# A four-layer gated attention and expert kernel: stacked masks in layer 0, half of the softmax sums in pairs on GpSimd, and a new planned order

## The chip, the cores and the metric

The kernel runs on one core of one Trainium2 chip. The core has five engines that run at the same time, each in the order of its own queue: TensorE (PE in the profile; its weight loads are the row PEld), VectorE (DVE), ScalarE (ACT), GpSimd (POOL) and SyncE (SP), which issues most of the transfers. The metric is the device time of one execution in microseconds (us), the median of several runs.

## The reference

There are 16 sequences of 128 tokens of width 128, and a context of 77 rows for each. Four layers follow each other, each an attention to the context and a feed-forward part, both gated into the token:

```
x = x + tanh(g_xattn[0]) * L0_xattn(layernorm(x), ctx, fside, mask)   # 16 heads of 8
x = x + tanh(g_ffn[0])   * L0_ffn(layernorm(x))                       # 8 experts, threshold router with capacity
x = x + tanh(g_xattn[1]) * L1_xattn(layernorm(x), ctx, key_mask)      # 16 heads of 8
x = x + tanh(g_ffn[1])   * L1_ffn(layernorm(x))                       # expert 0, layer norm
x = x + tanh(g_xattn[2]) * L2_xattn(layernorm(x), ctx)                # 16 heads of 64
x = x + tanh(g_ffn[2])   * L2_ffn(layernorm(x))                       # quantized
x = x + tanh(g_xattn[3]) * L3_xattn(layernorm(x), ctx, key_mask)      # 8 heads of 64
x = x + tanh(g_ffn[3])   * L3_ffn(layernorm(x))                       # 8 experts, best one for each token
```

Layer 0's attention, in short: the scores of a query with the 77 keys of its sequence get -1e9 where the mask (one value for each query and key) is 0. Their softmax is multiplied with `fside`, a weight for each query and key, and then with the values. The softmax divides by the sum of the exponents before that weighting. Layer 1's attention is alike, with a mask by keys and without the weighting.

Layer 0's router: a token's experts are ranked by their probability, those up to a mass of 0.9 are chosen, and each expert keeps the 256 tokens with the best value of probability less rank.

## The kernel before

The 16 sequences ("batches" here) are worked on in four groups of four. In `small_group` (layers 0 and 1) a group goes through a layer norm, a transposition, a product for its queries and one for its keys. Then, for each batch, `scores` (L820, L824) fills four strips of 128 queries x 308 (four heads of 77 keys) in PSUM. Each strip takes the mask terms first and then the product of queries and keys. Layer 0 has two mask terms for each strip: a 128x128 diagonal of 30512 and one of 5.578125, both half precision, times `pen0`, which is 0 or -32768 (L1190 makes it of the loaded mask). So a batch has eight mask products and four products of queries and keys, of two instructions each (L824).

The two halves of a batch's 16 heads then go each through: the maximum over the keys (L632), the difference (L634), the exponent (L839, ScalarE), in layer 0 the weighting with `fside` (L856, GpSimd or VectorE), and the sum over the keys (L844, VectorE, 8 heads x 77 keys). The sums of both halves together are inverted (L847), spread (L867), turned (L871) and copied (L875). The exponents, weighted in layer 0, are turned by TensorE in blocks of 128 (L650), copied back, and multiplied with the values (L885). That product is scaled with the inverted sums (L890), projected (L894) and added to the token (L693). The values pass through memory on their way (L793 stores, L797 loads), on SP's queue.

`norm` is the layer norm that all layers use: statistics on VectorE (L491), a few small instructions on GpSimd (`moments`, L498 to L503), two on ScalarE (L508, L510), again a few on GpSimd (`newton`, L514 to L520), and the scaling of the group's four batches on ScalarE (L526) or VectorE (L528).

`route_part` computes layer 0's routing of a group on VectorE: ranks (L1562 to L1571), the value that decides (L1572 to L1577), and its spreading over 16 columns (L1582) ahead of a transposition.

Other work fills the gaps of layer 0: the products of value and output weights with the context (L1486), which layers 2 and 3 need, and the keys of these layers (L1649).

All of this is written as pieces of work with a due time, an engine (or two to choose from, with a cost for each) and what each reads and writes. `Work.layout` plays the pieces through with these costs and writes them out in the order in which they would start. The order of every engine's queue, and the choice of engine, follows from that. `NUDGES` is a list of (first piece, number of pieces, hundredths) that moves due times, and `SLACK` makes VectorE look dearer by 0.5 in a choice. At run time an engine that reaches an instruction whose inputs aren't ready waits there.

Of the kernel before, what the change touches and what calls it, by code (L numbers as in the profile page):

```python
# [11 lines left out]
F32 = mybir.dt.float32  # L12
F16 = mybir.dt.float16
# [9 lines left out]
P = 128  # L23
B = 16
D = 128
# [34 lines left out]
WEIGH, WEIGH_COST = ("POOL", "DVE"), (1.3, 0.85)  # L60
SIDE, SIDE_COST = ("POOL", "DVE"), (1.3, 0.75)
# [12 lines left out]

NUDGES = (
    (206, 1, 230), (1755, 1, 143), (2153, 1, -200), (2640, 4, 268), (963, 1, -150), (960, 4, -257), (1701, 1, 117), (1797, 3,
    -30), (989, 1, -212), (1726, 8, -153), (2228, 4, 172), (2164, 2, -283), (1712, 1, -267), (1001, 1, -283), (1670, 6,
    -289), (1652, 1, -189), (813, 1, -237), (164, 8, -58), (162, 2, -260), (879, 6, 267), (1136, 1, -206), (141, 4, -145),
    (130, 1, 220), (738, 6, -165), (2242, 4, -104), (961, 1, -103), (2244, 8, -295), (1770, 2, 104), (488, 8, 333), (1339, 1,
    65), (466, 8, 69), (611, 4, 133), (1771, 1, -214), (65, 1, -226), (137, 4, -273), (2126, 1, -231), (567, 1, -156), (991,  # L80
    1, -231), (2046, 4, 47), (1919, 6, -283), (2452, 4, 299), (2195, 1, 100), (689, 1, -177), (1805, 2, 116), (332, 8, -352),
    (337, 8, -46), (956, 3, -22), (749, 8, -114), (2053, 8, 58), (2559, 1, -190), (501, 8, 217), (2655, 8, -72), (1935, 1,
    -263), (1015, 1, -100), (2403, 1, -88), (2766, 8, 120), (18, 8, 217), (399, 1, -14), (1548, 4, -46), (1542, 6, -252),
    (2445, 4, -44), (397, 8, 38), (849, 8, -70), (961, 1, -99), (1914, 2, -52), (1530, 4, -250), (869, 4, 264), (392, 1,
    156), (2068, 6, -52), (852, 4, 92), (1693, 2, -62), (991, 3, -232), (611, 8, 89), (869, 1, -276), (801, 1, 281), (2196,
    8, -30), (2416, 6, -273), (2216, 1, -248), (867, 5, -264), (2514, 5, -30), (798, 1, -157), (2351, 2, -317), (2685, 8,
    -69), (1474, 1, -91), (2385, 1, 256), (1690, 1, -24), (2175, 1, 121), (2054, 4, -47), (2514, 4, 127), (1485, 8, 274),
    (392, 2, 72), (2542, 6, -186), (1806, 8, 89), (987, 5, -196), (2633, 3, -250), (492, 8, -236), (406, 1, -183), (1838, 4,
    -210), (2352, 1, 274), (2199, 1, -277), (1610, 6, -212), (2547, 1, 242), (1723, 4, 60), (1676, 1, 271), (2059, 8, -270),
    (268, 8, -210), (1753, 8, 42), (2631, 2, -107), (1547, 1, -182), (1579, 4, 19), (377, 1, -73), (2080, 1, -38), (465, 1,  # L90
    -122), (2636, 3, 278), (995, 3, -161), (1571, 8, -123), (751, 1, -281), (249, 4, -311), (2634, 8, -121), (854, 6, 175),
    (798, 1, 75), (2614, 8, -397), (2289, 1, -240), (1009, 1, -99), (2536, 4, -99), (1299, 1, -270), (1024, 4, -270), (741,
    1, -114), (2480, 1, -296), (2417, 2, -257), (761, 1, -284), (2254, 2, -218), (971, 2, -251), (1011, 4, -314), (2837, 8,
    252), (1936, 4, 186), (2111, 8, -333), (1853, 1, 135), (600, 8, -33), (1839, 1, -241), (1855, 5, -100), (940, 1, -191),
    (769, 5, -205), (2002, 8, -31), (781, 4, -32), (756, 1, 62), (1072, 8, 12), (755, 2, -156), (2636, 2, 106), (1983, 8,
    -341), (1339, 1, -80), (1386, 1, -266), (859, 1, -136), (1416, 8, 137), (46, 4, 380), (756, 1, 143), (758, 1, -131),
    (1391, 2, 150), (2561, 1, -293), (940, 1, -187), (1841, 4, -270), (1507, 1, 86), (1946, 8, 10), (981, 1, -279), (446, 6,
    -301), (2680, 1, -210), (1864, 1, 190), (737, 2, -81), (1015, 1, 241), (1552, 3, 189), (2717, 4, -126), (18, 5, -237),
    (1001, 2, 288), (1022, 1, 163), (2195, 1, -59), (2536, 5, 258), (2458, 4, -80), (2490, 1, -296), (2494, 6, -198), (1560,
    4, -287), (1911, 5, -16), (864, 1, -297), (149, 3, 221), (1876, 4, 273), (1434, 4, -304), (2206, 3, -140), (41, 8, 260),  # L100
    (1443, 8, -98), (2206, 8, 75), (2039, 5, -256), (2046, 1, -229), (922, 1, -228), (985, 1, -170), (2074, 1, -269), (1418,
    4, -275), (2793, 5, -298), (2718, 4, -126), (1507, 1, -302), (869, 6, 233), (2206, 1, -48), (2034, 1, -65), (2068, 1,
    -220), (1851, 1, -301), (748, 4, 118), (1397, 8, 143), (1507, 1, 286), (1514, 1, -260), (375, 1, -253), (985, 1, -152),
    (2206, 1, -42), (2252, 1, -231), (1746, 8, 119), (2306, 1, 78), (1467, 6, -111), (1633, 1, 72), (1952, 1, -186), (981, 1,
    172), (411, 2, -92), (559, 8, 123), (397, 4, -18), (1219, 1, -151), (2480, 2, 127), (852, 1, -203), (1613, 2, 294),
    (2670, 8, -326), (2256, 1, -242), (953, 1, -194), (1058, 8, 100), (1952, 1, -49), (532, 1, -164), (1048, 4, -80), (1054,
    8, -91), (741, 1, -138), (2249, 8, 400), (987, 6, -205), (367, 6, -265), (803, 8, 294), (1414, 2, -267), (2897, 8, -243),
    (2492, 3, -282), (963, 1, 115), (1633, 1, -57), (1509, 1, -97), (1041, 2, 306), (806, 1, -238), (2008, 1, -88), (975, 1,
    -260), (920, 8, -208), (258, 8, -230), (491, 8, -48), (874, 1, -300), (607, 2, -81), (945, 1, -271), (789, 3, -171),
    (460, 1, 24), (791, 4, 298), (258, 2, 336), (741, 1, -71), (689, 1, -288), (2897, 4, 388), (1005, 1, -266), (959, 1,  # L110
    -21), (857, 1, 92), (431, 3, -191), (934, 1, -104), (801, 1, 296), (851, 4, -164), (854, 4, -222), (1851, 1, -94), (993,
    5, -152), (2101, 1, -233), (971, 1, 279), (972, 2, -204), (254, 1, -202), (1940, 8, -90), (869, 1, 75), (973, 1, -112),
    (1794, 3, -141), (2592, 4, -114), (973, 4, -248), (859, 6, -286), (2470, 1, -271), (1570, 2, -115), (533, 4, 282), (961,
    1, -279), (46, 8, -174), (969, 1, -122), (1612, 3, -61), (971, 2, -134), (2242, 5, 240), (2114, 8, -331), (1575, 4,
    -325), (2897, 4, -181), (2095, 4, -171), (276, 1, 275), (969, 1, -211), (1042, 1, -131), (1896, 4, 108), (969, 8, -121),
    (763, 1, -263), (2099, 3, -38), (2206, 4, -65), (1000, 4, -204), (2357, 4, 299), (579, 4, -325), (662, 3, -236), (2856,
    8, -367), (484, 8, 218), (2161, 1, -159), (223, 2, -98), (1570, 1, -262), (244, 8, -158), (222, 8, 52), (2175, 4, 50),
    (1503, 4, -114), (2473, 8, 89), (1843, 8, 137), (2215, 6, -274), (139, 1, 191), (1004, 6, -159), (748, 1, -271), (1838,
    4, -140), (2849, 1, 134), (999, 1, -226), (985, 4, -245), (2798, 5, -220), (922, 4, -286), (1052, 2, 119), (928, 5,
    -300), (981, 1, -222), (740, 8, -110), (1612, 4, -84), (1015, 2, -88), (996, 8, -105), (44, 8, -95), (2461, 5, 205),  # L120
    (1502, 4, -117), (2221, 4, -226), (485, 4, -357), (297, 4, -110), (1050, 4, -134), (2813, 1, -122), (1709, 1, -130),
    (1613, 8, 134), (2448, 8, 230), (969, 1, -243), (1004, 4, -257), (763, 1, -222), (2778, 4, 99), (2470, 8, 194), (689, 1,
    -221), (852, 4, -204), (741, 1, -194), (981, 1, -125), (1202, 6, -239), (894, 1, -144), (2159, 1, -243), (1609, 8, -138),
    (1466, 4, -384), (961, 1, -177), (991, 3, -168), (2474, 1, -277), (1057, 3, -180), (502, 1, -127), (2777, 5, 273), (1895,
    4, -78), (965, 5, -74), (995, 1, -230), (854, 4, -281), (154, 2, 382), (2206, 2, 85), (753, 2, -288), (2215, 6, -253),
    (969, 8, -361), (745, 4, 83), (974, 5, -239), (923, 6, -261), (983, 1, -186), (879, 1, 71), (625, 1, -169), (981, 1,
    -132), (140, 5, -185), (1802, 4, 47), (481, 8, 253), (2304, 2, -132), (1801, 5, -82), (2388, 6, 296), (743, 4, -136),
    (983, 6, 97), (872, 6, 146), (949, 5, -17), (865, 5, 90), (925, 5, -181), (136, 5, -180), (778, 1, -78), (803, 1, -263),
    (368, 1, 208), (2837, 8, 354), (1228, 1, 115), (2206, 1, -65), (1058, 1, -151), (793, 1, -302), (643, 1, 276), (2205, 3,
# [27 lines left out]
class Work:  # L157
# [50 lines left out]
    def nudged(self):  # L208

        due = [n["at"] for n in self.nodes]  # L210
        for first, count, hundredths in NUDGES:
            for i in range(first, min(len(due), first + count)):
                due[i] += hundredths / 100.0
# [1865 lines left out]
```

## Time and profile before

| | |
|---|---|
| median of 3 runs | 663.42 us (663.17 to 665.4) |
| the profiled execution | 666.49 us, span 664.8 us |
| mean granted TensorE clock | 0.976 |
| transfers | 117.47 MB, 177 GB/s over the span |

The span runs from the first instruction to the last; the execution's own time has 1.7 us more around it. A row of a group of instructions gives line, engine, operation, output and input with their shapes and the number of instructions, then the busy time and the mean duration of one in ns, then the idle time of the engine just before them and what ended it. Of the rows that the change touches, the difference (L634) and the maximum (L632) are the largest of VectorE: 112 instructions of 799 ns and of 780 ns.

### The profile page before, as it was taken

How to read it: one execution, taken by the hardware profiler on the slowest of the kernel's cores; microseconds unless marked ns; L12 is line 12 of the kernel's file. 1: busy time of each engine (PE TensorE's matmuls, PEld its weight loads, DVE VectorE, ACT ScalarE, POOL GpSimd, SP SyncE). 2: the span in 40 equal slices, each digit the busy share in tenths (PEclk: the TensorE clock that was granted, in tenths of full speed). 3: DMA queues.
4: the chain of work that ended last, by engine and by line, in shares of the span. 5: the costliest groups of instructions: out<-in, count | busy, mean ns of one | idle time of the engine just before them, and what ended most of it. 6: DMA issues, size and time to landing. Idle time of an engine off the chain costs nothing.

```text
span 664.8 us, 16370 instructions
## 1 busy us (share of the span) xinstructions
PE 604.2 (91%) x5795; PEld 435.4 (65%) x5795; DVE 524.9 (79%) x1224; ACT 427.2 (64%) x1131; POOL 305.8 (46%) x750
## 2 busy tenths in 40 slices
PE   3988998899999999988989999999999998799795
PEld 2555565565546778655646776687767776689795
DVE  3699999884675347999998998979999999878342
ACT  3545758577766656686687867647686758356463
POOL 8659445351000027624362735445445347645554
PEclk9888999999999999998999999999999999799898
DMA  8972473557445565489592757569964432666473
GB/s 228 272 233 68 150 183 110 150 165 207 144 131 159 160 187 144 140 239 296 160 269 88 217 169 227 188 175 315 292 178 130 122 98 83 198 180 181 125 225 84
DMA packets 169178, 117.47 MB, mean 177 GB/s; under 512 B 12649, under 2 KB 159984, under 8 KB 169098
## 3 DMA queue, kind: packets, MB, share of 16 engines
q1 hardware_dynamic: 166650, 112.55, 59.6%
q0 software_dynamic: 1728, 3.17, 1.3%
q8 instruction: 46, 0.75, 0.5%
q10 hardware_dynamic: 720, 0.71, 0.4%
q14 instruction: 34, 0.28, 0.1%
HBM read 61.43 MB, written 55.89 MB: 176 GB/s over the span
## 4 chain that ended last, share of the span: by engine, by line
PE 29%; DVE 13%; ACT 7%; POOL 7%; issue 2%; DMA 1%; another core or an unknown queue 1%; DVEq 0%; ACTq 0%; POOLq 0%
PE T L650 4%; PE h_ps L1927 4%; PE y L1001 4%; PE y L1942 3%; DVE pr L634 3%; PE q_ps L931 3%; DVE mx L632 2%; PE y L1062 2%; POOL pw L995 2%; PE h_ps L1041 2%; PE S L975 1%; DVE sb L988 1%; ACT xn L526 1%; PE O L885 1%; DVE ln_st L491 1%
## 5 line engine op out<-in xcount | busy, mean ns | idle before, releaser
L634 DVE TENSOR_TENSOR pr<-S,mx 128x616 f32<-128x616 f32 x112 | 89.5, 799 | 6.7
L632 DVE TENSOR_REDUCE mx<-S 128x8 f32<-128x616 f32 x112 | 87.4, 780 | 4.8 <-PE S L824 4.0
L650 PE MATMUL T<-ident,pw 128*128 128x128 f32 (+1 forms) x400 | 63.0, 284 | 6.5 <-POOL pw L995 4.3
L463 ACT COPY pT<-T 128x384 f32<-128x384 f32 x107 | 50.5, 479 | 26.6 <-PE T L650 26.0
L995 POOL TENSOR_TENSOR pw<-pr,rinv 128x616 f32<-128x616 f32 x34 | 41.2, 1216 | 53.5 <-DVE rinv L990 10.4
L650 PEld LDWEIGHTS T<-ident,pw 128*128 128x128 f32 (+1 forms) x400 | 45.9, 142 | 29.1 <-issue 12.0
L1001 PEld LDWEIGHTS y<-v,pT 128*128 128x128 f32 (+1 forms) x480 | 57.8, 191 | 9.6 <-issue 4.0
L1001 PE MATMUL y<-v,pT 128*128 128x128 f32 (+1 forms) x480 | 62.1, 278 | 1.5 <-ACT pT L463 1.1
L839 ACT ACTIVATE pr<-pr 128x616 f32<-128x616 f32 x64 | 45.9, 720 | 20.3 <-DVE pr L634 20.1
L856 POOL TENSOR_TENSOR pw<-pr,gp 128x616 f32<-128x616 f32 x26 | 36.0, 1387 | 37.2 <-ACT pr L839 23.9
L1811 DVE SCALAR_TENSOR_TENSOR token<-y,sc,token 128x128 f32<-128x128 f32 x96 | 32.9, 349 | 24.2 <-PE y L1806 21.7
L844 DVE TENSOR_REDUCE ss<-pr 128x8 f32<-128x616 f32 x64 | 49.6, 781 | 1.3 <-ACT pr L839 1.1
L931 PE MATMUL q_ps<-xT,wq 128*128 128x512 f32 x96 | 49.5, 613 | 0.8 <-DVE token L693 0.5
L463 ACT COPY vs<-f_ps 122x512 f32<-122x512 f32 (+3 forms) x57 | 33.1, 584 | 24.3 <-PE f_ps L1486 22.6
L1951 POOL DMA_INDIRECT out_x<-bo,row x30 | 29.8, 994 | 30.0 <-DVE bo L1946 15.1
L526 ACT ACTIVATE xn<-token,ln_b,ln_r 128x128 f32<-128x128 f32 x92 | 37.8, 486 | 7.4 <-POOL ln_b L520 7.3
L984 ACT ACTIVATE pr<-pr 128x616 f32<-128x616 f32 x48 | 34.0, 718 | 12.5 <-DVE pr L634 7.9
L657 ACT COPY pT<-T 128x128 f32<-128x128 f32 x104 | 28.2, 271 | 17.5 <-PE T L650 15.7
L1486 PE MATMUL f_ps<-vz,ctxT 128*122 128x512 f32 (+3 forms) x80 | 39.2, 602 | 0.1
L988 DVE TENSOR_REDUCE sb<-pr 128x8 f32<-128x616 f32 x48 | 37.4, 779 | 1.5 <-ACT pr L984 1.5
L975 PE MATMUL S<-k,q 64*64 64x77 f32 x1536 | 35.8, 235 | 0.9 <-DVE pr L634 0.8
L975 PEld LDWEIGHTS S<-k,q 64*64 64x64 f32 x1536 | 31.1, 136 | 7.7 <-issue 3.5
(338 smaller groups left out, 1490.4 us busy)
## 6 DMA issues: line engine op xcount, KB each, us to landing
v<-folded SPq DMA_DIRECT2D x48, 320.0 KB
vx<-apart SPq DMA_DIRECT2D x32, 320.0 KB
apart<-vz SPq DMA_DIRECT2D x32, 308.0 KB
rowsA<-blank SPq DMA_DIRECT2D x15, 516.0 KB
rowsZ<-blank SPq DMA_DIRECT2D x15, 516.0 KB
kept<-ks SPq DMA_DIRECT2D x24, 308.0 KB
k<-kept SPq DMA_DIRECT2D x12, 616.0 KB
folded<-vs SPq DMA_DIRECT2D x21, 308.0 KB
```

The source lines that it names most:

```text
L463: nc.scalar.copy(out, src)
L526: nc.scalar.activation(o[:, i, :], src()[:, i, :], AF.Identity, bias=mem["b"][:, i:i + 1], scale=mem["r"][:, i:i + 1])
L632: nc.vector.tensor_reduce(mx, S4, axis=AX.X, op=ALU.max)
L634: nc.vector.tensor_tensor(pr.rearrange("p (a c) k -> p a c k", a=2), S4, mx.unsqueeze(3).to_broadcast([P, 2, 4, SK]), ALU.subtract)
L650: nc.tensor.transpose(own[jkey][:n, c, :], flat[:, lo:lo + n], ident)
L839: nc.scalar.activation(own["pr", i, half], own["pr", i, half], AF.Exp)
L844: nc.vector.tensor_reduce(own["s", i][:, 8 * half:8 * half + 8], own["pr", i, half], axis=AX.X, op=ALU.add)
L931: nc.tensor.matmul(own["q_ps", c], lhsT=wq()[:, (c0 + c) * P:(c0 + c + 1) * P], rhs=mem["xT"], start=True, stop=True)
L975: nc.tensor.matmul(S[rows64, a, c * SK:(c + 1) * SK], lhsT=own["q"][at, c, i * P + 64 * b:i * P + 64 * b + 64], rhs=own["k"][at, c, i * SK ...
L988: nc.vector.tensor_reduce(s, own["pr", i], axis=AX.X, op=ALU.add)
L995: eng.tensor_tensor(own["pw", i], own["pr", i], own["rinv", i].unsqueeze(2).to_broadcast([P, 8, SK]), ALU.mult)
L1001: nc.tensor.matmul(own["y", i], lhsT=own[u + (i, "pT", c // 3)][:n, c % 3, :], rhs=own["v", i][:n, c, :], start=(c == 0), stop=(c == 4))
```

## The change

The masks of layer 0's groups 1 to 3 are loaded twice, to partitions 0 to 63 and 64 to 127, so that each partition half has the masks of 64 queries of all eight half batches. One weight `billions` holds both factors one above the other, 64 columns wide, and one product of 128 rows then gives the mask of 64 queries. A strip takes two such products, one for each half of its queries. Group 0 keeps the two diagonals. Groups 1 to 3 share one buffer for the loaded masks. The planner's cost of such a batch's scores is 1.12 where it was 1.76.

```
+    SIDES = lambda g: 2 if g else 1
-        m0.append(l0.tile([P, GB, SK], I32, name=f"m0_{g}"))
+        m0.append(None if g else l0.tile([P, GB, SK], I32, name="m0_0"))
-        pen0.append(l0.tile([P, GB, SK], F16, name=f"pen0_{g}"))
+        pen0.append(l0.tile([P, GB * SIDES(g), SK], F16, name=f"pen0_{g}"))
...
     def load_masks(g, eng):
-        eng.dma_start(out=m0[g], in_=io["mask0"][g * GB:(g + 1) * GB].rearrange("b q k -> q b k"))
+        if g:
+            m0[g] = l0.tile([P, 2 * GB, SK], I32, tag="m0", name="m0", bufs=1)
+            for lo in (0, 64):
+                eng.dma_start(out=m0[g][lo:lo + 64], in_=io["mask0"][g * GB:(g + 1) * GB].rearrange("b (h q) k -> q (b h) k", h=2))
+        else:
+            eng.dma_start(out=m0[g], in_=io["mask0"][g * GB:(g + 1) * GB].rearrange("b q k -> q b k"))
...
         for n, part in enumerate((30512.0, 5.578125)):
             nc.gpsimd.tensor_scalar(billion[n], ident, part, None, op0=ALU.mult)
+            lo = slice(64 * n, 64 * n + 64)
+            nc.gpsimd.tensor_scalar(billions[lo], ident[lo, lo], part, None, op0=ALU.mult)
...
                 terms = pen(g, i)
+                if layer == 0 and g:
+                    for out in strips:
+                        for half in range(2):
+                            rows64 = slice(64 * half, 64 * half + 64)
+                            nc.tensor.matmul(out[rows64], lhsT=billions, rhs=pen0[g][:, 2 * i + half, :].unsqueeze(1).to_broadcast([P, 4, SK]),
+                                             start=True, stop=False)
+                    terms = []
...
-            add(6 + g, "SP", 1.0, lambda g=g: load_masks(g, nc.sync), writes=[("m0", g), ("gp", g)], mb=0.315, parts=2)
+            if g == 2:
+                add(6 + g, "SP", 1.0, lambda g=g: load_masks(g, nc.sync), reads=[("pen0", g - 1)], writes=[("m0", g), ("gp", g)], mb=0.47, parts=3)
...
+            if g == 3:
+                add(6 + g, "SP", 1.0, lambda g=g: load_masks(g, nc.sync), reads=[("pen0", g - 1)], writes=[("m0", g), ("gp", g)], mb=0.47, parts=3)
```

The sums of the first eight heads, in layers 0 and 1, are made in two steps. GpSimd adds the keys in pairs (0 to 37 with 39 to 76, and key 38 to the first), and VectorE sums the 38 that remain. The second eight heads' sums are as before.

```
+                def paired(i=i):
+                    own["h", i] = wk.tile([P, 8, SK // 2], F32, tag="hs", name="hs", bufs=1)
+                    pr, n = own["pr", i, 0], SK // 2
+                    nc.gpsimd.tensor_tensor(own["h", i], pr[:, :, 0:n], pr[:, :, n + 1:SK], ALU.add)
+                    nc.gpsimd.tensor_tensor(own["h", i][:, :, 0:1], own["h", i][:, :, 0:1], pr[:, :, n:n + 1], ALU.add)
...
-                    nc.vector.tensor_reduce(own["s", i][:, 8 * half:8 * half + 8], own["pr", i, half], axis=AX.X, op=ALU.add)
+                    src = own["h", i] if half == 0 else own["pr", i, half]
+                    nc.vector.tensor_reduce(own["s", i][:, 8 * half:8 * half + 8], src, axis=AX.X, op=ALU.add)
...
-                add(th + 1, "DVE", 0.82 + 0.15 * half, sums, reads=[prk], writes=[sk], new=[("ss", sk)] if half == 0 else [])
+                pair = ui + ("h",)
+                if half == 0:
+                    add(th + 0.5, "POOL", 0.95, paired, reads=[prk], writes=[pair], new=[("hs", pair)])
+                add(th + 1, "DVE", 0.97 if half else 0.45, sums, reads=[prk] if half else [pair], writes=[sk], new=[("ss", sk)] if half == 0 else [])
```

The layer norm of layer 0's first group has its small instructions on VectorE, and its scaling is two pieces of two batches, each for ScalarE or VectorE:

```
+        few = nc.vector if first else nc.gpsimd
...
-            nc.gpsimd.tensor_tensor(d, st[:, :, 1], st[:, :, 4], ALU.subtract)
+            few.tensor_tensor(d, st[:, :, 1], st[:, :, 4], ALU.subtract)
...
+        if first:
+            add(at, "DVE", 0.9, moments, writes=[ln])
+            act(at, 0.45, guess, writes=[ln])
+            add(at, "DVE", 0.7, newton, writes=[ln])
+            for n, e in enumerate(FLEX):
+                half = range(2 * n, 2 * n + 2)
+                add(at, e, 0.85, lambda e=e, half=half: scaled(e, half), reads=list(skeys) + [ln], writes=[okeys[0] + (n,)], new=() if n else new)
```

In the routing of layer 0, the last five small instructions and the spreading may go to GpSimd or VectorE (the five compute what four did):

```
+            eng.tensor_scalar(rank, rank, 1.0, None, op0=ALU.add)
+            eng.tensor_tensor(R, pr(), rank, ALU.subtract)
+            eng.tensor_tensor(R, R, chosen, ALU.mult)
+            eng.tensor_scalar(chosen, chosen, 1.0, 1e9, op0=ALU.subtract, op1=ALU.mult)
+            eng.tensor_tensor(R, R, chosen, ALU.add)
...
+        add(at, "DVE", 2.3, before1, reads=[key], writes=[key])
+        add(at, "DVE", 1.45, before2, reads=[key], writes=[key])
+        add(at, both, (1.2, 0.9), before3, reads=[key], writes=[key])
+        add(at, both, (0.9, 0.45), spread, reads=[key], writes=[kx], new=[("xn", kx)])
```

The planner's costs change for some choices, `NUDGES` is a new list (443 entries instead of 582), and an entry with the number 0 adds to one piece's slack on the second of its two engines instead of moving its due time:

```
-WEIGH, WEIGH_COST = ("POOL", "DVE"), (1.3, 0.85)
-SIDE, SIDE_COST = ("POOL", "DVE"), (1.3, 0.75)
+WEIGH, WEIGH_COST = ("POOL", "DVE"), (1.25, 0.95)
+SIDE, SIDE_COST = ("POOL", "DVE"), (1.2, 1.2)
...
+            if count == 0:
+                odds[first] += hundredths / 100.0
...
-        add(at, FLEX, (1.6, 1.36), scaled, reads=list(skeys) + [ln], writes=okeys, new=new)
+        add(at, FLEX, (1.66, 1.75), scaled, reads=list(skeys) + [ln], writes=okeys, new=new)
-            add(at, FLEX, ((0.47, 0.55), (0.5, 0.45))[j], out, reads=[T], writes=[jkey])
+            add(at, FLEX, ((0.48, 0.55), (0.54, 0.55))[j], out, reads=[T], writes=[jkey])
-                    add(th + 0.1, ("POOL", "DVE"), (1.4, 0.85), weighted, reads=[prk, ("gp", g)], writes=[skey], new=[("pws", skey)])
+                    add(th + 0.1, ("POOL", "DVE"), (1.4, 1.15), weighted, reads=[prk, ("gp", g)], writes=[skey], new=[("pws", skey)])
```

## The prediction

> **What bounds the kernel now.** I read the page's busy shares first, then the busy time of each engine stage by stage, then the start in order of time, then the groups of the instructions that the diff touches.
>
> ```profile
> span 664.8 us, 16370 instructions
> PE 604.2 (91%) x5795; PEld 435.4 (65%) x5795; DVE 524.9 (79%) x1224; ACT 427.2 (64%) x1131; POOL 305.8 (46%) x750
> PE   3988998899999999988989999999999998799795
> DVE  3699999884675347999998998979999999878342
> ```
>
> TensorE is busy for 91% of the span, but the dips of the two rows lie in different slices, so one engine does not bound the whole. The stages, with columns length, PE, PEld, DVE, ACT, POOL, granted clock, DMA share, GB/s:
>
> ```profile
> 8.00:26.00 18.00, 12.45 (x50) 7.19 (x48) 9.47 (x23) 7.73 (x19) 14.05 (x43) 0.81 0.94 255
> 26.00:40.00 14.00, 10.70 (x96) 6.33 (x95) 13.29 (x25) 6.24 (x16) 7.11 (x8) 0.96 0.91 270
> 40.00:100.00 60.00, 55.02 (x497) 36.56 (x495) 56.34 (x119) 36.90 (x99) 37.38 (x70) 0.95 0.53 151
> 100.00:160.00 60.00, 55.18 (x471) 34.16 (x471) 51.65 (x117) 42.21 (x112) 25.54 (x46) 1.00 0.55 154
> 160.00:260.00 100.00, 100.00 (x432) 62.92 (x431) 54.22 (x142) 65.87 (x136) 15.11 (x46) 1.00 0.54 155
> 260.00:345.00 85.00, 74.83 (x757) 51.81 (x756) 80.47 (x176) 61.66 (x182) 41.12 (x104) 0.98 0.75 212
> 345.00:560.00 215.00, 208.53 (x2679) 154.57 (x2677) 196.59 (x408) 151.48 (x393) 102.06 (x310) 1.00 0.63 183
> 560.00:665.00 105.00, 85.91 (x822) 80.67 (x821) 61.97 (x216) 52.23 (x176) 57.03 (x105) 0.93 0.57 158
> ```
>
> Layer 0's attention (26 to 160) has VectorE at 121.3 of 134 us and TensorE at 120.9: both nearly full. The first expert stage (160 to 260) is TensorE alone, without a gap. Layer 1's attention (260 to 345) is VectorE's, 80.5 of 85, with TensorE idle for 10.2. From 345 to 560 TensorE idles 6.5 in 215 us; the last experts aren't touched.
>
> The start, in order of time (start, duration, engine, line):
>
> ```profile
> 5.09 0.87 DVE L491 BATCH_NORM_STATS2 ln_st<-token 128x6 f32<-128x128 f32 x4 [5.09 <-DMA token<-in_x]
> 8.86 0.21 POOL L498 TENSOR_TENSOR ln_d<-ln_st 128x4 f32<-128x4 f32 x1
> 9.46 1.42 POOL L501 TENSOR_SCALAR ln_w<-ln_sq 128x4 f32<-128x4 f32 x1
> 12.67 1.50 POOL L514 TENSOR_TENSOR ln_t<-ln_r 128x4 f32<-128x4 f32 x1
> 15.32 1.65 ACT L526 ACTIVATE xn<-token,ln_b,ln_r 128x128 f32<-128x128 f32 x4 [3.28 <-POOL ln_b L520]
> ```
>
> The first norm's statistics end at 5.96, but GpSimd starts on them at 8.86, and two of its instructions that usually take 0.2 take 1.4 and 1.5 while VectorE runs a long product with two SBUF inputs (L766). ScalarE gets the result at 15.32; the first scores follow at 20.45.
>
> ```profile
> L820 PE MATMUL S<-pen,billion 128*128 128x308 f16 x128 | 22.1, 312 | 3.5 <-DVE pr L634 3.5
> L885 PE MATMUL O<-pT,vx 128*32 128x128 f32 x640 | 27.6, 278 | 0.0
> L844 DVE TENSOR_REDUCE ss<-pr 128x8 f32<-128x616 f32 x64 | 49.6, 781 | 1.3 <-ACT pr L839 1.1
> L856 POOL TENSOR_TENSOR pw<-pr,gp 128x616 f32<-128x616 f32 x26 | 36.0, 1387 | 37.2 <-ACT pr L839 23.9 <-issue 10.6 <-POOL pw L856 1.4
> ```
>
> **The change, part by part.**
>
> *Masks stacked.* In 12 of layer 0's 16 batches, eight 128-column mask products become eight 64-column ones, in pairs on the two halves of the columns. Eight of the old ones take 1.26 us (at 96.67): seven steps of 0.136 and a last one of 0.31. No row shows a 128x64 product. The nearest is L885: 24 instructions of 278 ns each on 32 columns pass in 0.86 us, so column tiles do run side by side. If pairs do, four steps remain: 3 x 0.136 + 0.31 = 0.72, a gain of 0.54 a batch, 6.5 in all. If they don't, the gain is 0; and a further change of tile shape before each batch could cost the idle that the trace shows at such a change, 0.17 before L885's loads to 0.26 before L824's, so +2 to +3.1. I take -5.5: L885's row, less half of the cheaper switch (12 x 0.17 / 2 = 1.0). TensorE is full for the 100 us that follow, and the fold products (L1486) that fill layer 0's gaps can run there, so its saved work counts.
>
> On tile switches, the row is the 0.26 us of idle at L824. [...]
>
> The masks are also twice as large: two loads of 154 KB instead of one for groups 1 to 3, 0.47 MB at 255 to 270 GB/s, 1.8 us of transfer where the DMA share is above 0.9. Groups 2 and 3 load into one buffer, so their issues on SP's queue wait for the conversion of the group before; behind them stand the value stores and loads (L793, L797), and late next would be the O products. Conversion of 616 elements instead of 308: 0.31 us more on VectorE or 1.26 more on GpSimd, three times. I put both with the bounds of the next item.
>
> *The first norm on VectorE.* Eleven instructions of 0.2 (VectorE's L1574 to L1577 on 32 elements take 0.18 to 0.19, 0.22 from start to start) go into its idle time between 5.96 and 8.35, where it waits 2.39. Moments to 7.3, ScalarE's two after its table load (7.47) to 8.0, the rest to 9.2 instead of 15.28; the scaling split over two engines takes 0.8 instead of 1.65. The first scores could come some 7 us earlier. VectorE does 2.4 + 1.1 more, and its idle in 8 to 26 is 8.5. Bounds: 0, if the loads or the keys (L766 at 9.38, now later) hold it, and -7; I take -3, since a saturated VectorE behind it has the extra 3.5 to do.
>
> *Sums by pairs.* 32 times GpSimd adds 304 pairs and one odd column. Rows: L1823 takes 0.74 for 256 elements, L689 1.18 for 512, so 0.82 for 304, plus 0.20 (L499, 8 elements): 1.02, 32.6 us more on GpSimd. VectorE's reduction falls from 616 elements, 0.78, to 304; L1569 takes 0.42 for 256, so 0.47: 0.315 saved, 5.0 in each of the two attention stages. The sum of the first half has until the second half's sum (the reciprocal needs both), so its latency is hidden by the second half's maximum, difference and exponent, over 2 us. Without that cover it is 1.02 a batch, or 2.4 behind a weighting (L856) in GpSimd's queue; behind a waiting sum on VectorE stand the next maxima, and TensorE's scores wait for those.
>
> In layer 1, VectorE sets the pace with TensorE idle for 10.2: bounds 0 and -5, I take -4. In layer 0 TensorE's gain is counted above; VectorE's 5.0, and routing steps (L1574 to L1582, 5 instructions of 0.18 and one of 0.43, four times) that may go to GpSimd, only close TensorE's 13.1 us of gaps: 0 to -5, I take -2.
>
> *GpSimd against VectorE.* Where both want SBUF together, one waits: the copy L867 takes 1.29 beside a weighting (85.02) and 0.23 alone (98.09); L856 on VectorE takes 2.04 beside a long GpSimd instruction (64.41) and 0.79 else. The 32.6 us more bring more of this: 0 to +5; These two and the two of the start cost 1.06, 1.25, 1.2 and 1.3, together 4.8 in some 125 us of GpSimd's work (14 + 70 + 41), so 32.6 more bring 1.25; I take +1.5, as I looked only at a part of the instructions. [...]
>
> *New planning costs, due times and slacks* reorder everything on every queue, also where nothing else changes. I cost this at 0, bounds -5 and +11 (below).
>
> The sum: -5.5 - 3 - 4 - 2 + 1.5 = **-13.0**. The profiled execution took 666.49 (span 664.8 and 1.7 around it), so 653.5; it lies 3.07 above the median of 663.42, so **650.4**. The likeliest case's own range is 642 (masks at -6.5, start at -7, layer 0's gaps at -5: 8 less) to 659 (start at 0, meetings at +5, layer 1 at -2: 8.5 more).
>
> **The rivals.** *The halves run one after the other*: the mask gain is 0 and the switches cost 2, so 650.4 + 7.5 = 658. For it: no 128x64 row. Against it: L885. *The new order gives it back*: if TensorE in 345 to 560 idles as in 100 to 160 (8% instead of 3%), that stage grows by 10.8: 661. For it: 443 due times in place of 582, all new; against it: that stage's work is the same.
>
> *GpSimd's queue decides, and the kernel is slower.* GpSimd is busy for 70 of 134 us in 26 to 160; 16.3 for pairs, 5 for larger masks and up to 9 for routing make 100, a denser queue than anywhere now. Its weightings feed the transposes (4.3 us of waits at L650 are already for L995's), and the pair sums stand in the same queue. The point is where a half-sum makes VectorE stand for 13 / 32 = 0.41 us on average; at 0.65, half a weighting, it is +20.8 - 13 = +7.8: 671. Against it: GpSimd already waits 23.9 us for ScalarE at L856, so its queue has slack.
>
> **How the numbers follow.** Forecast 0.62, one-after-the-other 0.12, given back 0.09, GpSimd 0.17. This kernel's measurement tells 0.5% from no change, 3.3 us. Faster: 0.62 and 0.10 of the second, 0.72; same 0.02 + 0.09 = 0.11; slower 0.17. The range of 642 to 667 leaves out some 0.05 below and 0.13 above.
>
> **What would show it.** Mask products as 128*64, eight passing in about 0.7 us; the first scores near 14 instead of 20.45; the half-sum at 0.47; TensorE's idle in layer 1 down from 10.2 to about 6; GpSimd's busy time up by 30. Wrong if eight mask products still take 1.2, if VectorE shows waits for GpSimd's sums above 13 us in total, or if the stage from 345 to 560 grows.

## The result, and the profile after

The changed kernel takes 673.1 us (670.33 to 675.37), 1.0138 of before with an interval of 1.0102 to 1.0175: it is slower by 1.0 to 1.8%. The forecast was 650.4 with a range of 642 to 667. The profiled execution took 673.89 us, 7.4 more than that of before; spans 672.2 and 664.8.

The first lines of the page of after, in the order in which those of before were shown:

```profile
span 672.2 us, 16457 instructions
PE 611.7 (91%) x5795; PEld 438.3 (65%) x5795; DVE 523.1 (78%) x1241; ACT 420.5 (63%) x1101; POOL 354.5 (53%) x833
```

GpSimd has 48.7 us more. VectorE has only 1.8 less, and TensorE is busy for 7.5 us more although its mask products were to take some 6.5 us less. The stages follow (length, PE, PEld, DVE, ACT, POOL, granted clock, DMA share, GB/s; the granted clock is the share of its full speed at which TensorE ran):

```profile
8.00:26.00 18.00, 13.38 (x63) 7.95 (x63) 12.68 (x35) 7.46 (x17) 15.00 (x37) 0.94 0.98 246
26.00:40.00 14.00, 12.43 (x122) 8.27 (x121) 12.50 (x24) 7.75 (x20) 6.40 (x9) 0.96 0.89 251
40.00:100.00 60.00, 50.22 (x415) 32.76 (x417) 48.86 (x95) 32.70 (x84) 47.23 (x78) 0.80 0.49 131
100.00:160.00 60.00, 56.80 (x502) 34.02 (x495) 52.74 (x113) 40.81 (x114) 35.88 (x73) 0.97 0.61 168
160.00:260.00 100.00, 100.00 (x422) 62.42 (x421) 50.41 (x135) 65.95 (x130) 14.03 (x33) 1.00 0.60 175
260.00:345.00 85.00, 72.35 (x696) 51.12 (x695) 78.19 (x180) 56.67 (x165) 50.74 (x128) 0.96 0.63 180
345.00:560.00 215.00, 210.79 (x2657) 153.39 (x2656) 195.48 (x420) 146.57 (x380) 115.00 (x326) 1.00 0.64 188
```

From 40 to 100 TensorE and VectorE both do less than before (50.2 for 55.0, 48.9 for 56.3), and the granted clock falls from 0.95 to 0.80. No engine is full over these 60 us; they wait for each other. Layer 1 (260 to 345) has TensorE idle for 12.7 us where it was 10.2.

The operations themselves came out as priced. The groups of after by shape (out<-in, count, busy, mean ns, idle before):

```profile
L864 POOL TENSOR_TENSOR hs<-pr 128x304 f32<-128x304 f32 x32 | 27.6, 861 | 26.5 <-ACT pr L858 21.5 <-ACT vz L462 2.8 <-DVE ss L871 2.2
L871 DVE TENSOR_REDUCE ss<-pr 128x8 f32<-128x616 f32 x32 | 25.1, 784 | 0.4 <-ACT pr L858 0.4
L871 DVE TENSOR_REDUCE ss<-hs 128x8 f32<-128x304 f32 x32 | 14.7, 460 | 3.6 <-POOL hs L865 2.0 <-POOL pen3d L689 1.3
L833 PE MATMUL S<-pen,billions 128*64 128x308 f16 x96 | 10.2, 328 | 4.0 <-DVE pr L646 4.0
```

A half-sum takes 0.460 us, a pair add 0.861. VectorE waits for GpSimd at its half-sums for 3.3 us in all. So the rival that cost most in the forecast, VectorE standing behind GpSimd's sums (decided at 13 us), isn't what happened in this order. The largest difference from 40 to 100 lies in one place, on the timeline of after (start, duration, engine, line, operation, count, idle before):

```profile
53.56 4.85 POOL L696 TENSOR_SCALAR pen<-m,pen1d 128x1232 bf16<-128x1232 uint8 x1
...
60.77 0.73 PE L833 MATMUL S<-pen,billions 128*64 128x308 f16 x8
...
60.91 4.44 POOL L696 TENSOR_SCALAR pen<-m,pen3d 128x1232 bf16<-128x1232 uint8 x1
...
62.64 3.62 DVE L883 TENSOR_TENSOR pw<-pr,gp 128x616 f32<-128x616 f32 x2
65.30 0.30 POOL L897 COPY r<-rinvs 128x128 f32<-128x128 f32 x1
...
65.66 0.47 PE L901 MATMUL r_ps<-ident,r 128*128 128x128 f32 x1 [3.43 <-POOL r L897]
...
72.06 1.24 PE L833 MATMUL S<-pen,billions 128*64 128x308 f16 x8
```

Eight stacked mask products pass in 0.73 us, as forecast (0.72). Then GpSimd is held for 4.44 us by the conversion of layer 3's key mask. VectorE's two weightings beside it take 3.62 (the fastest one of this line takes 0.74), the copy of the inverted sums stands behind the conversion on GpSimd, and TensorE waits 3.43 us for that copy. After that the same eight products take 1.24 us, at a granted clock of 0.50 (from 65.6 to 80), where it was 1.00 from 58 to 62. The same trace also has the clock at 0.50 from 52 to 57, after a wait of 2.18 us (48.77 to 50.96).

The conversion alone doesn't make this jam. Before has the same two on GpSimd (4.44 us at 50.1 and 4.46 at 61.9), and TensorE stays at full clock from 60 to 80:

```profile
60.00:80.00 20.00, 18.61 (x172) 12.18 (x171) 17.91 (x36) 15.66 (x42) 13.36 (x26) 1.00 0.43 132
```

In after the copy that TensorE waits for has come to stand behind one of them.

The difference grows later. Layer 1's exponents, with first and last start, of before:

```profile
L839 ACT ACTIVATE pr<-pr x32: 701/717/762, 268.6 to 391.0; 128x616 f32<-128x616 f32 x32
```

and of after:

```profile
L858 ACT ACTIVATE pr<-pr x32: 705/717/762, 278.0 to 411.3; 128x616 f32<-128x616 f32 x32
```

The last of the first experts' output products starts at 276.2 in before and at 278.1 in after, 1.9 apart. But layer 1 begins 9.4 us later, and its last exponent comes 20.3 us later. Some of the late start is already there ahead of the expert stage: the router's cuts (on VectorE, the search for the limit of each expert) begin at 182.2 instead of 177.9, 4.3 us later. TensorE is full from 160 to 260 in both, so its busy share shows nothing of it; the order within that stage does. TensorE on the timeline of before:

```profile
249.50 3.73 PE L1806 MATMUL y<-w,h 128*128 128x128 f32 x32
253.07 1.88 PE L1486 MATMUL f_ps<-vz,ctxT 128*122 128x512 f32 x4
254.79 0.60 PE L610 MATMUL tp<-ident,xn 128*128 128x128 f32 x4
```

and of after:

```profile
257.00 5.65 PE L1849 MATMUL y<-w,h 128*128 128x128 f32 x48
262.49 0.38 PE L791 MATMUL v_ps<-w,ctxT 128*77 128x128 f32 x2
262.92 1.16 PE L1849 MATMUL y<-w,h 128*128 128x128 f32 x8
264.33 2.13 PE L1849 MATMUL y<-w,h 128*128 128x128 f32 x16 [0.26 <-DVE token L1854]
266.30 1.40 PE L622 MATMUL tp<-ident,xn 128*128 128x128 f32 x4
```

`tp<-ident,xn` is the transposition that opens layer 1's first group; it needs that group's expert outputs (y). Before begins the outputs at 210.3 and does fold products (f_ps, values and output weights with the context) between them, the last from 257.4. After starts its last fold at 233.6, begins the outputs at 223.5, and opens layer 1 at 266.3 instead of 254.8. Ahead of that transposition stand 184 of the 256 output instructions in after, and 144 in before. The same products in another order, and layer 1, which TensorE does not fill, starts 9 to 11 us later.

### The profile page after: what moved, and what is told of

Its sections match the earlier page's. It is cut to its first block, busy times and chain, and to the rows that moved or that the text cites. A ratio compares the mean times of both kernels' runs of the same rounds, so it can differ in the third digit from the quotient of the medians.

```text
span 672.2 us, 16457 instructions
## 1 busy us (share of the span) xinstructions
PE 611.7 (91%) x5795; PEld 438.3 (65%) x5795; DVE 523.1 (78%) x1241; ACT 420.5 (63%) x1101; POOL 354.5 (53%) x833
## 4 chain that ended last, share of the span: by engine, by line
PE 62%; POOL 13%; DVE 11%; ACT 5%; issue 4%; DMA 4%; SPq 0%; POOLq 0%; DVEq 0%; ACTq 0%
PE T L662 7%; PE f_ps L1520 7%; PE y L1031 6%; PE q_ps L961 5%; PE h_ps L1824 4%; PE k_ps L1692 4%; PE S L1005 3%; PE h_ps L1970 3%; PE y L1849 3%; PE O L915 2%; PE y L1985 2%; PE y L1092 2%; ACT xn L529 2%; DVE mx L644 2%; PE S L843 2%
## 5 line engine op out<-in xcount | busy, mean ns | idle before, releaser
L1025 POOL TENSOR_TENSOR pw<-pr,rinv 128x616 f32<-128x616 f32 x40 | 48.5, 1215 | 59.5 <-DVE rinv L1020 30.2
L662 PE MATMUL T<-ident,pw 128*128 128x128 f32 (+1 forms) x400 | 66.5, 291 | 9.1 <-POOL pw L1025 7.7
L462 ACT COPY pT<-T 128x384 f32<-128x384 f32 x101 | 47.9, 480 | 33.5 <-PE T L662 32.8
L662 PEld LDWEIGHTS T<-ident,pw 128*128 128x128 f32 (+1 forms) x400 | 47.8, 146 | 32.2 <-POOL pw L1025 12.4
L529 ACT ACTIVATE xn<-token,ln_b,ln_r 128x128 f32<-128x128 f32 x94 | 38.6, 482 | 11.9 <-POOL ln_b L521 10.2
L462 ACT COPY vs<-f_ps 122x512 f32<-122x512 f32 (+3 forms) x54 | 31.5, 585 | 19.0 <-PE f_ps L1520 15.3
L864 POOL TENSOR_TENSOR hs<-pr 128x304 f32<-128x304 f32 x32 | 27.6, 861 | 26.5 <-ACT pr L858 21.5
L883 POOL TENSOR_TENSOR pw<-pr,gp 128x616 f32<-128x616 f32 x22 | 30.5, 1387 | 20.4 <-ACT pr L858 20.4
L778 POOL TENSOR_TENSOR kx<-ks,headmask 128x1232 f32<-128x1232 f32 x7 | 15.7, 2238 | 42.5 <-DVE token L1854 42.5
```

Source lines behind the costliest of these rows:

```text
L462: nc.scalar.copy(out, src)
L529: nc.scalar.activation(o[:, i, :], src()[:, i, :], AF.Identity, bias=mem["b"][:, i:i + 1], scale=mem["r"][:, i:i + 1])
L662: nc.tensor.transpose(own[jkey][:n, c, :], flat[:, lo:lo + n], ident)
L1025: eng.tensor_tensor(own["pw", i], own["pr", i], own["rinv", i].unsqueeze(2).to_broadcast([P, 8, SK]), ALU.mult)
```

## The experiments

Before was measured again beside every group of experiments, on the same chip, and the ratio is against those runs. Their median was 663.5 (e1 to e4), 668.9 (e5 to e8), 668.8 (e9 to e12), 663.3 (e13 to e16) and 663.1 (e17, e18). Times inside a profile are given as they stand, so those of e5 to e12 come from chips on which before takes some 5 us longer.

**Parts taken out of after, and put into before (e1 to e4).**

e1 leaves the pair adds out of after:

```
-                    own["h", i] = wk.tile([P, 8, SK // 2], F32, tag="hs", name="hs", bufs=1)
...
+                    pass
-                    src = own["h", i] if half == 0 else own["pr", i, half]
+                    src = own["pr", i, half]
```

> The changed kernel in its own order, with the pair additions left out and the first half's sums made on VectorE from all 77 keys: 33 us less on GpSimd, 10 us more on VectorE. If the pair additions in GpSimd's queue cost the time (theory GpSimd), most of the 9.5 us over the kernel before goes away: 660 to 666. If the new order of all queues costs it (theory order), VectorE's 10 us come on top or nothing changes: 671 to 680.

Measured 1.0158 [1.0139, 1.0177]. The pair adds aren't the loss in this order; what they gain, if anything, the intervals don't separate from nothing.

e2 gives after the two 128-column products and single mask loads back (the branch `if layer == 0 and g:` and the second load are gone).

> The changed kernel in its own order, with two 128-column products a strip for layer 0's masks, as in the kernel before, and single loads of the masks. TensorE has 12 x 0.54 = 6.5 us more work. If this work counts, 677 to 680; if TensorE waits for others there anyway, 672 to 675; below 671 if the doubled loads and conversions were a cost.

Measured 1.0089 [1.0067, 1.0111]. The median of 670.0 us lies in the third range: stacking does not gain in this order, and without it the kernel is some 0.5% faster, with intervals that just overlap. The doubled masks delay the start in both orders: the first scores come at 18.23 in after and 16.50 in e2, and at 23.73 in e3 (next) and 22.24 in before.

e3 puts the stacked masks into before, with two shared buffers for the loaded masks:

```
+            m0[g] = l0.tile([P, 2 * GB, SK], I32, tag="m0", name="m0", bufs=2)
+            for lo in (0, 64):
...
+                if layer == 0 and g:
```

> The kernel before in its own order, with the stacked masks alone. Both theories allow a gain by TensorE's saved 6.5 us: 657 to 660. If it is hidden behind VectorE in layer 0, or eaten by the doubled loads and conversions, 662 to 666.

Measured 0.9997 [0.9978, 1.0017]. In its profile TensorE is busy for 52.07 us of 40 to 100 (55.02 in before), and the router's cuts begin at 176.7 instead of 177.9: of some 6.5 us less work (12 x 0.54), 1.2 arrive there, and nothing at the end.

e4 puts the pair adds into before, right behind the first half's exponent:

```
                     nc.scalar.activation(own["pr", i, half], own["pr", i, half], AF.Exp)
+                    if half == 0:
+                        own["h", i] = wk.tile([P, 8, SK // 2], F32, tag="hs", name="hs", bufs=1)
...
+                    src = own["h", i] if half == 0 else own["pr", i, half]
```

> The kernel before in its own order, with the pair additions alone, each put into GpSimd's queue where the first half's exponent is issued. Theory GpSimd: slower than before, 668 to 675. Theory order: the parts do no harm, 658 to 664.

Measured 1.0125 [1.0106, 1.0145]. The cuts begin 10.5 us late (188.4); behind the first experts nothing more is lost. The waits of e4 in 26 to 160 (engine, line, waited for, us, times, longest):

```profile
PEld T L650 <- POOL pw L862: 7.3, 8, 2.6
DVE ss L850 <- POOL hs L844: 4.9, 7, 1.5
PE T L650 <- POOL pw L862: 4.3, 4, 2.3
```

VectorE waits 4.9 us for the pair sums, about what they save in layer 0, and the weightings queued behind them hold the transposes. VectorE's six weightings take 1.45 us each, 1.03 in before, beside a busier GpSimd. In an order that isn't made for them, the pairs cost time through GpSimd's queue, as in the rival that I had at 0.17, although VectorE stands for 0.34 us a half-sum (10.8 / 32 in both layers), below the 0.41 that I had set.

**The lists of due times (e5, e6, e8, e9).** e5 is after with every due-time entry of before carried over to the same piece, and the planner costs of before that don't belong to the changed work; e6 carries them over from layer 1 on alone; e8 and e9 are after and before with an empty list:

```
-NUDGES = (
...
+NUDGES = ()
```

> The kernel after with the due times of before, each carried over to the same piece of work, and the five planner costs of before that have nothing to do with the changed work (weightings, side work, norm scaling, block copies). The new pieces (pair adds, the second scaling, the last routing steps) have no due-time change. Theory order (the new due times and costs are what loses): about the time of before less a part of what was saved, 655 to 664. Rival structure (pairs and doubled masks lose with any order, as pairs lost 8.4 in the order of before): 668 to 676. If it is above 676 the old times don't fit the new costs, and it tells nothing.

Measured 1.0462 [1.0428, 1.0496], the range that tells nothing.

> The kernel after, with its own due times up to the end of the first expert stage and those of before, carried over piece by piece, from layer 1 on; costs are those of after. The kernel after lost 6.5 us against before between the end of the first experts and the last scores of layer 3. Theory order: that loss goes, 666 to 668, and the stretch takes about 303 instead of 309.6. Rival structure: it stays, 672 to 676, since layer 1 has the pair adds in both.

Measured 1.0386 [1.0351, 1.0421], outside both ranges.

> The kernel after with an empty list of due-time changes: the costs, pieces and code stay. It shows what the list of after is worth to it. Theory order (the list of after is a poor one): not more than 10 us slower than after, below 683. Rival structure (the list of after is as well fitted as the one of before): 685 to 705.

Measured 1.0448 [1.0414, 1.0481], where the rival had it.

> The kernel before with an empty list of due-time changes. Without its list the kernel after takes 1.0448 of before. Theory order (the work of after is no worse than that of before, only its list fits it less well): before without its list is at 1.045 or above, 693 or more where before takes 663.5. Rival structure (the added GpSimd work costs 1 to 1.5% with any order): 1.03 to 1.035, 683 to 687.

Measured 1.0458 [1.0421, 1.0496], where the order theory had it. Without lists the two kernels take the same time, each in the order that its own costs give; the work of the change shows no gain and no loss there. Before's list takes off 4.4%, after's 3.0%. In e5, before's list takes nothing off. That due times fit only the costs that they were found with would explain it, but isn't shown.

**Order alone (e10).** After's order, engine choices, norm and routing, with the edits of e1 and e2 together.

> The order, engine choices, first norm and routing of after, but all sums whole on VectorE from 77 keys (the pair adds are left out) and two 128-column mask products with single mask loads. Theory order: what is left of the loss is the order's alone, ratio 1.008 to 1.013 (669 to 672). Rival structure (pairs and stacked masks are the loss): 0.997 to 1.003 (661.5 to 665.5).

Measured 1.0142 [1.0103, 1.0181], like after itself. So pairs and stacked masks together neither add to the loss nor take from it. The first norm and the routing are still in, but both lie ahead of the router's cuts, and e10's cuts begin at 177.4, no later than before's 177.9. What is lost is lost behind them, where only the order and the choice of engines differ. Layer 1's exponents in e10:

```profile
L850 ACT ACTIVATE pr<-pr x32: 701/717/760, 273.2 to 406.3; 128x616 f32<-128x616 f32 x32
```

and in e1:

```profile
L858 ACT ACTIVATE pr<-pr x32: 700/717/761, 275.5 to 409.8; 128x616 f32<-128x616 f32 x32
```

They start 4.8 and 2.5 us earlier than in after (278.0). Yet the last scores of layer 3 start at 587.8 and 587.1, in after at 587.7, and in before at 579.2. So with the order that after has behind the experts, an earlier start of layer 1 gains nothing.

**Where in the order (e11, e13, e14).** These three fix the order by a rank and an engine for each piece:

```
+RANK = (
...
+ON = (
...
+            i = min((i for i in ready if can(i)), key=lambda i: RANK[i])
...
-        for i in self.layout():
+        for i in self.ranked():
```

e11: after's order until the first experts end, before's behind.

> The kernel after, its own order for all work that it plans to start before the first expert stage ends, and behind that the order and the engine choices of before, each piece of work matched, with the pair adds of layer 1 issued right behind the exponent as in e4. Theory order (after loses its 6.5 us in layers 1 to 3 by the order of the work there, not by the pair adds): the stretch from the end of the first experts to the last scores of layer 3 takes 303 to 305 instead of 309.6, and the kernel 665 to 668 (1.002 to 1.007). Rival structure (the pair adds cost it there): 308 or more, 671 to 675 (1.011 to 1.017).

Measured 1.0142 [1.0098, 1.0185], where the rival had it: a miss of the order theory as I had put it. The stretch that was to take 303 to 305 takes 313.7 (276.3 to 590.0). But layer 1's first exponent is at 276.1 in it, so before's order behind the experts also starts late. That led to the late start as theory.

e13: before's order already from the cuts on, so with the expert stage.

> The kernel after, its own order up to the point where the cuts of layer 0's router begin, and behind that the order and engine choices of before, now with the first expert stage. Theory late start (after puts key and fold products ahead of the expert outputs of group 0, so layer 1's first exponent comes at 278.0 instead of 268.6 and that delay is carried to the end): the first exponent of layer 1 at 269 to 273, and the kernel 1.002 to 1.007 of before (665 to 668 where before takes 663.5). Rival own pieces (after loses through pairs and masks that any later order must bear): 1.010 to 1.018 as in e11.

Measured 1.0071 [1.0045, 1.0097]; the first exponent is at 273.9, 5.3 us later than in before, and so are the cuts (183.2 instead of 177.9). Both lie just outside the theory's ranges. About half of the loss is gone, with all of the change's work still in.

e14: before, with nothing of the change but the expert stage's pieces in the order of after.

> The kernel before, nothing of the change in it but one thing: the pieces of work that it plans between the start of the cuts and the end of the first experts' outputs stand among themselves in the order of after. Theory late start: the first exponent of layer 1 comes 8 to 10 us later than in before (about 277) with the first experts ending within 2 us of before, and the kernel is 1.008 to 1.016 of before (669 to 674). Rival: this stage has slack, TensorE is full in both orders, and the ratio is 0.997 to 1.004.

Measured 1.0122 [1.0076, 1.0168]. Its exponents:

```profile
L1061 ACT ACTIVATE pr<-pr x32: 701/717/763, 279.3 to 400.4; 128x616 f32<-128x616 f32 x32
```

The experts end 3.3 us later than in before (279.5), a little more than I expected, and the cuts begin 3.0 later; but layer 1 starts 10.7 later, its last exponent is 9.4 later and the last scores of layer 3 are 9.5 later (588.7). This stage's order alone makes a loss of after's size, in a kernel that has before's order everywhere else. It is not the whole account of after: there e1 and e10 started layer 1 earlier and gained nothing. How after's loss divides between the expert stage and the order behind it stays open.

**GpSimd's jam (e7, e17).**

```
-        nc.gpsimd.tensor_scalar(t.rearrange("p b k -> p (b k)"), mask, sub, digit, op0=ALU.subtract, op1=ALU.mult)
+        nc.vector.tensor_scalar(t.rearrange("p b k -> p (b k)"), mask, sub, digit, op0=ALU.subtract, op1=ALU.mult)
```

> The kernel after, with the two conversions of the key masks (4.85 and 4.44 us on GpSimd at 53.6 and 60.9) issued on VectorE at the same places. Theory jam (in layer 0 GpSimd's queue holds weightings and pair adds behind these two, TensorE waits and falls to half clock): the granted clock in 60 to 80 rises from 0.62 to above 0.8 and the kernel gains 3 to 5 us: 668 to 670. Rival order: the two are only one of many waits, and VectorE has to do them instead: 672 to 675.

Measured 1.0155 [1.0116, 1.0193]. The jam does go; 60 to 80 in after:

```profile
60.00:80.00 20.00, 15.57 (x107) 10.73 (x109) 15.39 (x34) 9.23 (x26) 18.56 (x37) 0.62 0.12 33
```

and in e7:

```profile
60.00:80.00 20.00, 17.24 (x146) 12.23 (x146) 15.32 (x40) 11.37 (x34) 14.91 (x32) 0.85 0.15 44
```

The cuts begin 2.5 us earlier (179.7) and layer 1's exponents too (275.5), and none of it arrives at the end.

> e13 (own order of after up to the cuts, order of before behind) with the two conversions of the key masks on VectorE instead of GpSimd, as in e7. Of after's loss e13 kept 0.7%, with the cuts beginning at 183.2 instead of 177.9. Theory jam (what is left is layer 0's, and half of it is GpSimd's queue behind these two conversions): the cuts begin 2 to 4 us earlier and the ratio falls to 1.001 to 1.005. Rival: the cuts come earlier, but nothing reaches the end, as in e7: 1.006 to 1.010.

Measured 1.0045 [1.0021, 1.0069]; the cuts begin at 179.7. With before's order from the cuts on, some of the gain may stay; the intervals of e13 and e17 overlap, so that isn't shown. What makes the last 0.45% is open; it lies in after's order of layer 0 or in what e17's later order still waits for.

**Gains that could be kept (e12, e15, e16, e18).** e12 is e3 with the first group's small norm instructions on VectorE:

```
+        few = nc.vector if key == ("xn", 0, 0) else nc.gpsimd
```

> The order of before with the stacked masks and the first group's small norm instructions on VectorE, nothing else: the two parts of the change that give GpSimd nothing between 26 and 160. With the first scores 3 to 5 us earlier and 5.5 us less mask work on TensorE, theory bound (layer 0 is bound by TensorE's work) gives 655 to 658. Rival chain (layer 0 is held by the chain through VectorE and GpSimd, and what is saved ahead of it is waited away before the first experts): 660 to 664.

Measured 0.9976 [0.9955, 0.9997], where the rival had it: 1.6 us below before, with an interval that overlaps those of e3 and e18. The first scores come at 22.34, not earlier than before's 22.24: on VectorE the last five norm instructions stand behind the key product (10.74 to 12.17).

e15 and e16 move the key and fold products of e12's expert stage 25 and 12 us back in the order.

> The kernel of e12 (order of before, stacked masks, first norm on VectorE) with the key and fold products for layers 2 and 3 that it plans between 203 and 262 us, and their copies and stores, each 25 us later in the order, so that the expert outputs of group 0 and layer 1 start earlier. Theory late start turned round: the first exponent of layer 1 comes 8 to 14 us before e12's (which has it 2.1 before that of before), TensorE's idle time in layer 1 is filled by the moved products, ratio 0.980 to 0.992. Rival: layers 1 and 2 take their pace from VectorE, whose copies of the moved products now stand in layer 1: 0.995 to 1.005.

Measured 1.071 [1.0659, 1.076].

> As e15 with the same products 12 us later in the order. Theory late start: the first exponent of layer 1 some 5 to 8 us before e12's, ratio 0.985 to 0.994. Rival: 0.995 to 1.002.

Measured 1.0323 [1.0274, 1.0373]. Both are plain misses. Layer 1's first exponent is later, not earlier (294.6 and 276.0, against 266.5 in e12), and in e15 no engine is busy for half of 250 to 265. Between 245 and 330 ScalarE waits for stores of values to leave their buffer:

```profile
ACT vz L694 <- DMA apart<-vz: 11.1, 5, 3.3
```

So moving all fillers back may run into something that they share with layer 1; that, and which buffer or queue it would be, wasn't settled. In before's order a later start costs (e14); that an earlier start than before's is to be had isn't shown.

e18 has the pairs in layer 1 alone, in before's order, with e12's norm.

> The order of before, the first group's small norm instructions on VectorE, and the pair adds in layer 1 alone (layer 0 has whole sums). In e4, with pairs in both layers, the loss was all in layer 0. My prediction's step for layer 1 (VectorE sets the pace there, its 5 us come off): 0.990 to 0.994. Rival (the 5 us of VectorE's work lie on no path that sets the end): 0.996 to 1.002.

Measured 0.9993 [0.9978, 1.0009]. VectorE in layer 1 (268 to 391), in before:

```profile
L844 DVE TENSOR_REDUCE ss<-pr 128x8 f32<-128x616 f32 x31 | 23.9, 780 | 0.4 <-ACT pr L839 0.2
```

and in e18:

```profile
L851 DVE TENSOR_REDUCE ss<-pr 128x8 f32<-128x616 f32 x15 | 11.7, 782 | 0.8 <-ACT pr L840 0.8
L851 DVE TENSOR_REDUCE ss<-hs 128x8 f32<-128x304 f32 x15 | 7.0, 465 | 5.7 <-POOL hs L845 5.7
```

The sums fall from 23.9 to 18.7 us, and VectorE then waits 5.7 for GpSimd at the same place. The saved work became a wait of its own length, in this order. In after it didn't: VectorE waits 1.3 us at the 16 half-sums of layer 1 that start from 278 to 411. There the pairs leave VectorE less to do, and e1 shows no gain from it either.

## Why the prediction was wrong

The step that failed is the one costed at nothing: "New planning costs, due times and slacks reorder everything on every queue". With the first norm and the routing still in, the new order cost 1.42% (e10), 9.4 us at 663.4. My upper bound of +11 held it, but I took 0, between ends 16 us apart, without a row that was near it. Which piece of the order costs how much in after stays open; what the runs show is that the order of the expert stage alone can cost 1.22% (e14). The profile could have shown that this stage sets when layer 1 starts: TensorE is full from 160 to 260, and VectorE, busy for 54 of 100, waits 21.7 us for the experts' outputs. The rival that had the right word for it, "the new order gives it back", named only 345 to 560 as the place, and TensorE's idle time as the sign; there after's TensorE idles 4.2 us instead of 6.5. From the first to the last scores of layers 2 and 3, after takes 219.2 us where before takes 216.0 (368.5 to 587.7, 363.2 to 579.2), with more of TensorE's work in it (210.6 for 204.3).

The savings were the second failure. *Masks, -5.5*: the duration was right (0.73 for eight) and the worth was 0 (e3), and not above 0 in after's order (e2). The reason that I gave, TensorE is full for the 100 us that follow, doesn't carry: layer 0 in front of them did not get shorter by what TensorE saved. *First norm, -3*: the first scores of after do come earlier, 18.23 for 22.24, 4 of the 7 hoped for. It was never run alone; with the masks it is worth 1.6 us (e12), which isn't clear of the masks alone (e3), and there the scores came no earlier than in before. *Layer 1's pairs, -4*: in before's order 5.2 us of VectorE's work went, as worked out, and 5.7 of new wait came (e18); in after's order the wait didn't come, and the work that went gained nothing (e1). That VectorE is busy for 80 of 85 us was read as VectorE setting the pace; neither run bears that out. *Layer 0's gaps, -2*: with the pairs in before's order it is +8.4 (e4). *Meetings of GpSimd and VectorE, +1.5*: e4's six weightings alone lost 2.5 (6 x 0.42), so this was too low for that order; in after it wasn't measured apart. The +5 that the range up to 659 takes for them was an estimate that no run shows.

Of the signs that I named, the products and the half-sum came out as said. The first mask products (17.07, not 14, for 20.45; the scores themselves 18.23 for 22.24), layer 1's idle (12.7, not 6) and GpSimd's busy time (48.7 more, not 30; the pair adds are 27.6 + 8.0 of it) did not. Of the signs of being wrong, the first two didn't come. The time is close to the slower rival's 671, but by luck, not by its cause: the half-sums made VectorE stand for 0.10 us each (3.3 / 32), a quarter of the deciding point.

## What to carry to other kernels

When a change replaces a tuned order with a new one, price the order first: here a list of due times is worth 3.0 to 4.4%, while the edited instructions gave 0.24% at best (e12) and cost 1.25% where the pairs were put into before's order (e4). In a stage where one engine is full, look not at its busy share but at which of its pieces opens the next stage, and whether work that nobody waits for stands ahead of it. Before counting work taken off a busy engine, look whether the same engine will then wait for the helper that took it.

## What the runs showed of the hardware

TensorE's granted clock was lower behind its long waits. From 40 to 100 its busy time fell from 55.0 us in before to 50.2 in after, and the granted clock from 0.95 to 0.80; after waits of 2.18 and 3.43 us the clock was 0.50, and eight products took 1.24 us instead of 0.73. Less work alone didn't lower it: in e3, with the stacked masks in before's order, TensorE is busy for 52.07 us of these 60 and the clock is 0.97.

GpSimd took some five times as long as VectorE to convert masks: 4.44 us against 0.85 (e7) for 128x1232 from uint8, 2.3 against 0.47 for 128x616 from int32.
